# Softmax attention on one Trainium2 core: a bound check in place of the row-maximum pass, with scores in four row strips and weighted sums in four column strips

## The chip, the cores and the metric

The kernel runs on one core of one Trainium2 chip. The metric is the device time of one execution in microseconds (us). On one core there is no second die to compare with, so a run is called fast when it lies within 1.5% of the fastest run of the same kernel; a kernel that was run only once has the state "unknown". All matrices are fp32. The profile also gives the clock that the throttle granted to TensorE, as a share of full speed. Its lines name the engines: PE is a matmul on TensorE and PEld a weight load, DVE is VectorE, ACT is ScalarE, POOL is GpSimd, SP is SyncE. A row strip is a quarter of TensorE's array, 32 of its 128 rows; a column strip is 32 of its 128 columns. In a line, `32*128` is the rows and columns of the array that a matmul uses.

## The reference, cut to what matters

The network takes x of (2, 128, 64, 64) through four residual layers. Layers 1 and 2 (convolutions, and a quaternion product in the Fourier domain) are the same before and after the change. Layers 0 and 3 contain softmax attention over all S = 64 x 64 = 4096 tokens:

```python
# layer 0: 4 heads of 32 channels, q and k of length 1
q1, q2, k1, k2 = map(l2norm_tokens, (q1, q2, k1, k2))
attn1 = jax.nn.softmax(jnp.einsum('bhnc,bhmc->bhnm', q1, k1) * temperature, axis=-1)
out1 = jnp.einsum('bhnm,bhmc->bhnc', attn1, v)
# ... a second attention over channels, output convolutions

# layer 3: 8 heads of 16 channels
a = jnp.einsum('bhcq,bhck->bhqk', q, k) / jnp.sqrt(jnp.float32(C))
a = jax.nn.softmax(a, axis=-1)
o = jnp.einsum('bhqk,bhck->bhcq', a, v)
```

A softmax usually subtracts each row's greatest score, so that the exponentials can't overflow. Its result is the same without the subtraction, as long as no exponential and no sum of them overflows or vanishes.

`l2norm_tokens` divides by `sqrt(sum(t*t, axis=2))`, where axis 2 is that of the tokens: each channel, not each token, has length 1 over the 4096 tokens. For one channel no product of a q and a k exceeds 1, so a score of layer 0 is at most 32 times the temperature, which is 1 here.

## The kernel before

Keys are taken in 32 tiles of 128, queries in 8 blocks of CH = 512 columns (one PSUM bank in fp32). For each head a score matmul puts 128 keys x 512 queries into PSUM, ScalarE takes the exponential into SBUF, and a sum matmul multiplies it with the values, and with ones for the softmax's denominator.

A head needs only 16 or 32 rows of contraction, but every score matmul contracts all 128 rows: q stands in a block that is zero in the rows of the other heads. A first pass over all scores finds the row maxima, which then enter the scores as one more row of the contraction.

```python
def _max_pass(nc, pool, ps_pool, ident, blocks, q, k, hs, d, nh):
    # ... for each query tile qt, key chunk kc and pair of heads p:
                ps = ps_pool.tile([128, 2, CH], F32, tag="sp", name="ps_max")
                for jj in range(2):
                    nc.tensor.matmul(ps[:, jj, :], qm[:, p + jj, :],
                                     k[:, kc * CH : (kc + 1) * CH], start=True, stop=True)
                nc.vector.tensor_reduce(pm[:, p : p + 2, qt, kc], ps, AX.X, ALU.max)
    # ... the maxima are turned and written into a row of q

def _attn_pass(nc, p_pool, ps_pool, acc_pool, blocks, q, k, values, hs, d, nh, done):
    # ... multiply(qb, kt, p, w): two sum matmuls, in different column strips of one accumulator
    for qb in range(NCH):
        # ... qm: q of this block, zero in the rows of the other heads
        for kt in range(NQT):
            for p in range(0, nh, 2):
                ps = ps_pool.tile([128, 2, CH], F32, tag="sp", name="ps_s")
                for jj in range(2):
                    nc.tensor.matmul(ps[:, jj, :], k[:, kt * 128 : (kt + 1) * 128],
                                     qm[:, p + jj, :], start=True, stop=True)
                w = p_pool.tile([128, 2, CH], F32, tag="weights", name="weights")
                nc.scalar.activation(w, ps, AF.Exp)
                waiting.append((qb, kt, p, w))
                if len(waiting) > 1:
                    multiply(*waiting.pop(0))
```

The generators are woven: in layer 0 the maxima pass of the first half with the convolutions for the values, and later maxima passes with the attention pass before them. PSUM, into which the matmuls write, is used as eight banks: three score buffers of two banks each, and two accumulators.

## Time and profile before

| | before |
|---|---|
| median time, us (3 runs) | 16939.77 (16937.05 to 16952.22) |
| TensorE busy | 97% |
| ScalarE busy | 21% |
| VectorE busy | 29% |
| layer 0 / layers 1 and 2 / layer 3, us of the profiled run | 5860 / 1426 / 9684 |

TensorE is the bound. The lines of the profile, and what they say, stand in the prediction below.

### The profile page before, as it was taken

To read this page: it belongs to the slowest core of one execution; us is meant where nothing else is said; L and a number is where in the kernel's file an instruction comes from. 1 tells how busy PE (TensorE), PEld (TensorE's weight loads), DVE (VectorE), ACT (ScalarE), POOL (GpSimd) and SP (SyncE) were. 2 spreads that over 40 slices of the span, in tenths; PEclk is the share of its full clock that TensorE was granted. 3 is DMA by queue.
4 is the path that set the end of the run, shared out by engine and by line. 5 is a ranking of instruction groups with operands and counts; after the bars stand their busy time and mean duration, and the time that the engine had idled before them with its cause. 6 is when DMAs were issued, how large, how long until landed. Compare 5 with 4: busy or idle time off the path is not lost.

```text
span 16969.8 us, 116126 instructions
## 1 busy us (share of the span) xinstructions
PE 16401.0 (97%) x50778; PEld 6151.0 (36%) x50778; DVE 4966.5 (29%) x4328; ACT 3536.5 (21%) x3820; POOL 468.1 (3%) x1029
## 2 busy tenths in 40 slices
PE   8999998999999788899999999999999999999999
PEld 3433322443332246644333333333333333333222
DVE  4432201352320352267422222322223222221000
ACT  1022232102223201100122222222222222222333
POOL 0000000000000100000000000000000000000000
PEclk9999998999999887889999999999999999999999
DMA  0000000000000015400000000000000000000000
GB/s 19 0 0 0 0 0 0 0 0 0 0 1 0 2 17 83 68 2 0 1 1 1 1 1 1 1 1 1 1 1 1 1 1 1 1 1 1 1 1 1
DMA packets 142859, 90.89 MB, mean 5 GB/s; under 512 B 4752, under 2 KB 137616, under 8 KB 142352
## 3 DMA queue, kind: packets, MB, share of 16 engines
q1 hardware_dynamic: 141056, 80.52, 2.9%
q8 instruction: 399, 6.54, 0.2%
q10 hardware_dynamic: 1296, 2.95, 0.1%
q14 instruction: 108, 0.88, 0.0%
HBM read 78.87 MB, written 4.19 MB: 5 GB/s over the span
## 4 chain that ended last, share of the span: by engine, by line
PE 63%; ACT 1%; issue 1%; DVE 0%; POOL 0%; ACTq 0%; DMA 0%; DVEq 0%; POOLq 0%; SPq 0%
PE ps_max L175 22%; PE ps_s L224 21%; PE ps_acc L207 12%; PE ps_freq L735 2%; PE ps_bank L718 1%; PE ps_bank L707 1%; PE ps_bank L614 1%; PE ps_t L585 1%; ACT yt L715 0%; PE ps_bank L622 0%; PE ps_bank L795 0%; PE ps_bank L764 0%; PE ps_bank L572 0%; PE ps_bank L668 0%; PE ps_sp L887 0%
## 5 line engine op out<-in xcount | busy, mean ns | idle before, releaser
L182 DVE TENSOR_REDUCE max_part<-ps_max 128x2 f32<-128x1024 f32 x3072 | 3765.1, 1226 | 7590.7 <-PE ps_max L175 7589.5
L224 PE MATMUL ps_s<-q_block,k 128*128 128x512 f32 x12288 | 5888.7, 602 | 18.6 <-POOL q_block L163 18.6
L175 PE MATMUL ps_max<-k,max_block 128*128 128x512 f32 x12288 | 5842.6, 610 | 11.2 <-ACT weights L232 5.9
L232 ACT ACTIVATE weights<-ps_s 128x1024 f32<-128x1024 f32 x3072 | 3144.9, 1024 | 10551.5 <-PE ps_s L224 10551.4
L175 PEld LDWEIGHTS ps_max<-k,max_block 128*128 128x128 f32 x12288 | 2164.5, 189 | 3662.1 <-issue 2459.3
L224 PEld LDWEIGHTS ps_s<-q_block,k 128*128 128x128 f32 x12288 | 2253.2, 190 | 3313.2 <-issue 2870.5
L207 PE MATMUL ps_acc<-weights,vt 128*32 128x512 f32 (+1 forms) x12288 | 3258.9, 609 | 1.7 <-ACT weights L232 1.7
L207 PEld LDWEIGHTS ps_acc<-weights,vt 128*32 128x32 f32 (+1 forms) x12288 | 497.5, 116 | 2331.9 <-issue 2310.4
L311 PE MATMUL ps_acc<-xn,wc 128*128 128x512 f32 x1440 | 631.3, 594 | 0.0
L470 DVE RECIPROCAL rec<-rec 64x512 f32<-64x512 f32 x32 | 107.0, 3345 | 1468.2 <-ACT rec L469 1468.2
L163 POOL COPY max_block<-q 16x128 f32<-16x128 f32 (+1 forms) x768 | 233.4, 304 | 9288.2 <-PE ps_max L175 8846.6
L885 DVE COPY u<-ps_acc 128x512 f32<-128x512 f32 x32 | 22.1, 690 | 1482.8 <-PE ps_acc L207 1482.8
L311 PEld LDWEIGHTS ps_acc<-xn,wc 128*128 128x128 f32 x1440 | 272.4, 190 | 342.1 <-issue 342.1
L718 PE MATMUL ps_bank<-consts,yt 128*128 128x99 f32 x1024 | 185.5, 338 | 86.2 <-ACT yt L715 86.2
L735 PEld LDWEIGHTS ps_freq<-e,w_r 128*32 128x32 f32 x4224 | 255.8, 153 | 19.0 <-issue 12.7
L735 PE MATMUL ps_freq<-e,w_r 128*32 128x16 f32 x4224 | 259.9, 212 | 2.2 <-DVE e L725 2.2
L735 PE MATMUL ps_freq<-e,w_i 128*32 128x16 f32 x4224 | 255.4, 212 | 0.0
L735 PEld LDWEIGHTS ps_freq<-e,w_i 128*32 128x32 f32 x4224 | 253.0, 157 | 2.8 <-issue 1.4
L163 POOL COPY q_block<-q 17x512 f32<-17x512 f32 (+1 forms) x192 | 115.8, 609 | 4833.5 <-PE ps_s L224 3802.4
L718 PEld LDWEIGHTS ps_bank<-consts,yt 128*128 128x128 f32 x1024 | 160.6, 239 | 219.1 <-ACT yt L715 218.9
L607 DVE SCALAR_TENSOR_TENSOR X<-g,w,X 128x4096 f32<-128x4096 f32 x50 | 234.7, 4693 | 1.8
L725 DVE COPY e<-ps_bank 128x396 f32<-128x396 f32 x128 | 143.4, 1120 | 307.6 <-PE ps_bank L718 307.6
(176 smaller groups left out, 3012.2 us busy)
## 6 DMA issues: line engine op xcount, KB each, us to landing
w_r<-in_L_conv_kr_w SPq DMA_DIRECT2D x16, 528.0 KB, 12.3
w_r<-in_L_conv_kr_x SPq DMA_DIRECT2D x16, 528.0 KB, 11.8
w_r<-in_L_conv_kr_y SPq DMA_DIRECT2D x16, 528.0 KB, 11.9
w_r<-in_L_conv_kr_z SPq DMA_DIRECT2D x16, 528.0 KB, 11.9
w_i<-in_L_conv_ki_w SPq DMA_DIRECT2D x16, 528.0 KB, 5.4
w_i<-in_L_conv_ki_x SPq DMA_DIRECT2D x16, 528.0 KB, 7.7
w_i<-in_L_conv_ki_y SPq DMA_DIRECT2D x16, 528.0 KB, 10.0
w_i<-in_L_conv_ki_z SPq DMA_DIRECT2D x16, 528.0 KB, 11.9
```

The lines of the kernel that those rows point to most:

```text
L163: nc.gpsimd.tensor_copy(block[hs * j : hs * j + rows, j, :], q[hs * j : hs * j + rows, cols])
L175: nc.tensor.matmul(ps[:, jj, :], qm[:, p + jj, :], k[:, kc * CH : (kc + 1) * CH], start=True, stop=True,)
L182: nc.vector.tensor_reduce(pm[:, p : p + 2, qt, kc], ps, AX.X, ALU.max)
L207: nc.tensor.matmul(acc[0][r : r + hs, :], values(kt, p + jj), w[:, jj, :], start=(kt == 0), stop=(kt == NQT - 1),)
L224: nc.tensor.matmul(ps[:, jj, :], k[:, kt * 128 : (kt + 1) * 128], qm[:, p + jj, :], start=True, stop=True,)
L232: nc.scalar.activation(w, ps, AF.Exp)
L311: nc.tensor.matmul(out, wc[:, t, grp * C : (grp + 1) * C], xn[:, c * ROWS + t // 3 : (c + 1) * ROWS + t // 3, t % 3 : t % 3 + W], start=(t ...
L585: nc.tensor.matmul(t3[:, lo // 4, : (hi - lo) * C], xt[:, 3 + u, :], xt[:, u + lo : u + hi, :].rearrange("p k c -> p (k c)"), start=(u == ...
L607: nc.vector.scalar_tensor_tensor(xi, g[:, i : i + H, j : j + W], w8[:, s : s + 1], xi, ALU.mult, ALU.add)
L614: nc.tensor.matmul(pv, t9[:, k, :], t2[:, c * ROWS + k : (c + 1) * ROWS + k, 2 : W + 2], start=(k == 0), stop=False,)
L718: nc.tensor.matmul(pe[:, r * 3 * FW : (r + 1) * 3 * FW], yt[:, r * 128 : (r + 1) * 128], k["fwd_w" if fh == m else "fwd_w_mirror"], start= ...
L735: nc.tensor.matmul(out.rearrange("p (x c) -> p x c", c=2), ws[n][:, :, gq * FW + fw], ef[:, :, 1 - n : 3 - n], start=(n == 0), stop=(n == 1),)
```

## The change

The intent is to spend less TensorE time per head. First, the maxima pass goes. An upper bound of the scores is computed on the device instead (32 x |temperature| in layer 0; in layer 3 the largest |q| times the largest |k| of each channel, summed over a head). If it is over 60, a branch at the end runs the old kernel as the general path and overwrites the output. On the given inputs the bound is 32 in layer 0 and at most 21.6 in layer 3, so the branch isn't taken.

Second, no zero-padded q: four heads lie 32 rows apart, and each score matmul contracts only its own 32 rows. The four matmuls of a turn use four row strips of the array and write to four PSUM banks. Third, the sums use four column strips of 32, four heads at once. The core of the diff, with cuts marked:

```diff
+LIMIT = 60.0
+def _attn_four(nc, p_pool, ps_pool, q, k, multiply):
+    waiting = []
+    for qb in range(NCH):
+        for kt in range(NQT):
+            ps = [ps_pool.tile([128, 2, CH], F32, tag="sp", name="ps_s") for _ in range(2)]
+            for j in range(4):
+                rows = slice(32 * j, 32 * j + 32)
+                nc.tensor.matmul(
+                    ps[j // 2][:, j % 2, :],
+                    k[rows, kt * 128 : (kt + 1) * 128],
+                    q[rows, qb * CH : (qb + 1) * CH],
+                    start=True, stop=True,
+                )
+            w = []
+            for p in range(2):
+                w.append(p_pool.tile([128, 2, CH], F32, tag="weights", name="weights"))
+                nc.scalar.activation(w[p], ps[p], AF.Exp)
+            waiting.append((qb, kt, w))
+            if len(waiting) > 1:
+                multiply(*waiting.pop(0))
...  layer 0: values and ones in two accumulators
+            for n in range(2):
+                for j in range(4):
+                    rows = slice(32 * j, 32 * j + 32)
+                    nc.tensor.matmul(
+                        accs[n][rows, :],
+                        ones if n else vt[:, kt, rows],
+                        w[j // 2][:, j % 2, :],
+                        start=(kt == 0), stop=(kt == NQT - 1),
+                    )
...  layer 3: values and ones of a head share one strip of 32 columns
+            for j in range(4):
+                i = j % 2
+                nc.tensor.matmul(
+                    acc[0][32 * j : 32 * j + 32, :],
+                    vt[:, kt, 2 * t + j // 2, i : i + 2, :].rearrange("p a d -> p (a d)"),
+                    w[j // 2][:, i, :],
+                    start=(kt == 0), stop=(kt == NQT - 1),
+                )
...  layer 3: the bound, once for each sample and half of the heads
+        nc.vector.tensor_reduce(mq, q, AX.X, ALU.max, apply_absolute_value=True)
+        nc.vector.tensor_reduce(mk, k, AX.X, ALU.max, apply_absolute_value=True)
+        nc.vector.tensor_mul(mq, mq, mk)
+        ps = sp()
+        nc.tensor.matmul(ps[:, 0, 0:1], head_sum, mq, start=True, stop=True)
...  the end of the kernel
+            nc.vector.tensor_scalar(within, top, LIMIT, None, ALU.is_le)
+    ok = nc.values_load(within[0:1, 0:1])
+    with tc.If(ok == 0):
+        _general(tc, a, out)
```

A "turn" below is one key tile with four heads in the changed kernel: four score matmuls, two exponentials of 128x1024, and the sums of the turn before (four matmuls in layer 3, eight in layer 0).

## The prediction

> **What bounds the kernel now.** I read the busy shares first, then the chain that ended last, then the costliest groups, then a table of the span by stage, and last the order of time inside one attention loop. The page:
>
> ```profile
> PE 16401.0 (97%) x50778; PEld 6151.0 (36%) x50778; DVE 4966.5 (29%) x4328; ACT 3536.5 (21%) x3820; POOL 468.1 (3%) x1029
> ...
> PE 63%; ACT 1%; issue 1%; DVE 0%; POOL 0%; ACTq 0%; DMA 0%; DVEq 0%; POOLq 0%; SPq 0%
> ...
> L182 DVE TENSOR_REDUCE max_part<-ps_max 128x2 f32<-128x1024 f32 x3072 | 3765.1, 1226 | 7590.7 <-PE ps_max L175 7589.5
> L224 PE MATMUL ps_s<-q_block,k 128*128 128x512 f32 x12288 | 5888.7, 602 | 18.6 <-POOL q_block L163 18.6
> L175 PE MATMUL ps_max<-k,max_block 128*128 128x512 f32 x12288 | 5842.6, 610 | 11.2 <-ACT weights L232 5.9
> L232 ACT ACTIVATE weights<-ps_s 128x1024 f32<-128x1024 f32 x3072 | 3144.9, 1024 | 10551.5 <-PE ps_s L224 10551.4
> L207 PE MATMUL ps_acc<-weights,vt 128*32 128x512 f32 (+1 forms) x12288 | 3258.9, 609 | 1.7 <-ACT weights L232 1.7
> ```
>
> TensorE is busy 97% and hardly waits; VectorE and ScalarE wait for it. Three groups hold 15.0 of 17.0 ms: the scores for the row maxima (L175), the scores again for the softmax (L224), the weighted sums (L207). The program has 24 head-samples (4 heads x 2 in layer 0, 8 x 2 in layer 3), each 8 query blocks x 32 key tiles = 256 score matmuls, 6144 in all; the trace has 12288, so one fp32 matmul is two passes. The stages (start:end, length, then each engine's busy us; PEclk and DMA last):
>
> ```profile
> 0.00:229.00 229.00, 164.66 (x338) 66.51 (x338) 81.50 (x100) 41.69 (x84) 27.05 (x21) 1.00 0.10 35
> 229.00:880.00 651.00, 646.10 (x1622) 294.00 (x1622) 323.33 (x280) 42.41 (x93) 26.43 (x74) 1.00 0.00 0
> 5860.00:6272.00 412.00, 331.36 (x809) 153.60 (x808) 270.14 (x129) 19.33 (x34) 84.92 (x36) 0.87 0.01 2
> 6272.00:7286.00 1014.00, 840.30 (x10696) 643.61 (x10696) 255.44 (x396) 131.41 (x242) 0.97 (x3) 0.74 0.45 70
> 7311.00:8189.00 878.00, 878.00 (x2047) 388.74 (x2046) 628.47 (x516) 0.00 (x0) 33.47 (x116) 1.00 0.00 0
> 15450.00:16960.00 1510.00, 1499.72 (x4127) 424.58 (x4128) 41.38 (x37) 524.08 (x512) 19.28 (x32) 1.00 0.01 1
> ```
>
> Layer 0 ends near 5860, layers 1 and 2 take 412 + 1014 = 1426 us, layer 3 is 7286 to the end, 9684 us. The row 7311:8189 is a pure maxima pass: 878 us / 2048 = 0.429 us a pass, so a full fp32 score matmul costs 0.858 us. The last row is a pure attention pass; inside it:
>
> ```profile
> 16899.68 1.98 PE L224 MATMUL ps_s<-q_block,k 128*128 128x512 f32 x4
> 16900.22 0.19 PEld L224 LDWEIGHTS ps_s<-q_block,k 128*128 128x128 f32 x1 [0.24 <-issue]
> 16901.59 0.14 PEld L207 LDWEIGHTS ps_acc<-weights,vt 128*32 128x32 f32 x4 [0.76 <-issue]
> 16901.60 1.05 PE L207 MATMUL ps_acc<-weights,vt 128*32 128x512 f32 x4
> 16901.76 1.02 ACT L232 ACTIVATE weights<-ps_s 128x1024 f32<-128x1024 f32 x1 [1.87 <-PE ps_s L224]
> 16902.58 0.30 PEld L224 LDWEIGHTS ps_s<-q_block,k 128*128 128x128 f32 x2 [0.84 <-PE ps_s L224]
> ```
>
> One turn (two heads of a key tile) runs 16899.68 to 16902.58, 2.90 us. Two score matmuls are 4 passes x 0.43 = 1.72. The two sums, in different 32-column strips, have 4 passes in 1.05 us including about 0.16 of pipeline tail: two strips run at once, 0.86 for both. The remaining 2.90 - 1.72 - 0.86 = 0.32 is two changes of array shape, drain and first weight load included. ScalarE works 1.02 and waits 1.87.
>
> **What the Trainium skill says.** "TensorEngine Tiling (Array Packing)", Key Properties: tiles load weights and multiply independently, but changing the tiling mode drains the engine. The trace agrees: the strips above overlap, and 0.32 us goes at the two changes. "TensorE: Matmul & The Clock Gate", Part 3: four row tiles of K=32, N=512 measured 3.07 times faster, three column tiles 2.38; a K=32 matmul alone costs what a K=128 one does. No run here shows row tiles yet, nor four strips at once, nor fp32 in them. "PSUM — Partial Sum Buffer", bank collisions: different row tiles must not write one bank at a time; the changed code gives each of the four strips its own bank, and then has room for only one and a half turns (six score banks). "ScalarE: Activation LUTs", What ACT_TABLE_LOAD costs: 186 ns + 0.833 ns an element is 1.04 us for 1024, less some 93 ns when back to back; the trace has 1.024, and where a 0.60 us ACTIVATE has a follower at once, that one starts 0.49 to 0.50 us later. So an exponential stream can run at 0.93 to 1.02 us apiece.
>
> **The change, part by part.** I evaluated the bound on the given inputs: 32 in layer 0 and at most 21.6 in layer 3, under the limit of 60. The branch is not taken, so the general path costs only a flag test, some 10 us.
>
> 1. *Maxima pass removed.* 6144 x 0.858 = 5272 us of TensorE, all on its path; VectorE's 3765 us of reductions and the zero-padded blocks go too, worth nothing by themselves. Layer 0's convolutions for the second attention and the values were woven into the first maxima pass (229:880): 651 - 512 x 0.858 = 212 us of them stays and stands alone now, with some waits: 240 a sample.
>
> 2. *Scores from four row strips.* A turn is now four heads of a key tile. If the strips overlap, four score matmuls cost 0.86 us, not 3.43. An unknown is the weight load: 128 columns take 0.11 us from one start to the next (two loads within 0.30 us, one is 0.19). Four strips loading in parallel add nothing; eight loads strictly one after another would make 0.75 + 0.86 = 1.6. I take 1.0, near parallel.
>
> 3. *Sums from four column strips.* Layer 3: four at once 0.86. Layer 0: values and ones apart, eight matmuls, two rounds, 1.72.
>
> 4. *Turns.* Layer 0: 1.0 + 1.72 + 0.32 = 3.04, TensorE bound; with small waits 3.1; 2 x 256 turns = 1587. Layer 3: TensorE 1.0 + 0.86 + 0.32 = 2.18; ScalarE two exponentials, 1.86 to 2.05; and a loop through both: end of an exponential, sums 0.92, shape change 0.2, scores 1.0 and 0.26 latency, two exponentials, together 4.24 to 4.43 over two turns, 2.1 to 2.2 each. All three nearly agree; I take 2.25; 4 x 256 turns = 2304.
>
> 5. *Edges of layer 3.* Each of 32 query blocks ends with a copy, two selecting matmuls and a reciprocal of 3.36 us that holds one of three score buffers, so about two turns run short. Before it cost 1510/8 - 64 x 2.90 = 3 us a block; now I estimate 5: 160. Each of four half-layers needs its projections unhidden (16 us, as at 7295 to 7311 before) and a new abs-max of q and k, which the built order puts before the first score: 29 each, 116. Statistics, normalizing and values per sample 28: 56. Sum 332; layer 3 is 2304 + 332 = 2636.
>
> 6. *Rest of layer 0.* First prologue 229; woven work now alone 2 x 240; output projections 2 x 118 (2827 to 2945 before); second sample's normalizing and convolutions 67 + 124; block edges 16. Sum 1152; layer 0 is 1587 + 1152 = 2739, against 5860.
>
> Total 2739 + 1426 + 2636 + 10 = 6811 of span; the timed runs are about 30 us below the profiled one, so about 6790, rounded to 6800. TensorE drops from 16.4 ms to perhaps 6; ScalarE stays at 3.4 and becomes a second bound in layer 3.
>
> **Rivals.**
> - *Strips overlap fully and exponentials run back to back.* Turns 2.05 and 2.9: 1024 x 0.2 + 512 x 0.2 = 307 less, about 6500. For it: strips in pairs begin within 0.01 us above. Against: in-order TensorE and only three score buffers of two banks.
> - *Weight loads serialize.* Scores 1.6 a turn: 1536 x 0.6 = 920 more at worst, part hidden in layer 3 by ScalarE: 7400 to 7700. For it: the 0.11 us spacing, which is for one row group; against: the skill's 3.07 times.
> - *Strips run only in pairs.* The profile shows two strips, never four. Sums then cost 1.72 in layer 3 and 3.44 in layer 0: 1024 x 0.86 + 512 x 1.72 = 1760 more, 8500. If the scores paired too, another 1300.
> - *ScalarE becomes the bound and the weaving is missed.* The unwoven parts together cost about what rows 1, 5 and 6 say; if waits doubled them, 300 to 400 more.
>
> **Range and chances.** The maxima alone are 31% of the time, and even the pairs-only case is far below 16940. Main doubt is how well four fp32 strips overlap. 6800 with 6350 to 7700 for 8 in 10: the low end is the first rival with smaller edges, the high end the second. Faster by 2% 0.98, within 0.01, slower 0.01 (the branch taken or a failure).
>
> **What would show it.** In the changed profile: no maxima group and no large reduction; score matmuls of form 32*128, still 12288, four starting nearly together; 16384 sums of form 128*32. A turn in layer 3 near 2.2 us with exponentials 1.0 us apart, one in layer 0 near 3.0 with ScalarE waiting about a third. Layers 1 and 2 at 1426. ScalarE busy near 3.5 ms, over half of the span. Wrong if the four strips' starts are 0.1 us or more apart (weight loads), if third and fourth sums start 0.43 us after the first (pairs), if the granted clock falls below 1.0 in the attention stages, or if a turn in layer 3 has TensorE and ScalarE both idle.

## The result, and the profile after

The changed kernel is correct and takes **6548.69 us** (median of 4 runs, 6520.2 to 6567.97), against 16944.6 for the kernel before in the same rounds. The ratio is 0.3864, with a 95% interval of 0.3854 to 0.3873. Here and below a ratio is the mean time of one kernel's fast runs over that of the other's fast runs of the same rounds, so it isn't quite the ratio of the quoted medians. The prediction of 6800 was 4% too high, and the result lies inside its range.

From the page of the changed kernel: each engine's busy time and share, then the costliest attention groups (count, then busy us and mean ns of one, then the idle time before them):

```profile
PE 5979.5 (91%) x42571; PEld 2201.9 (34%) x42571; DVE 1148.3 (18%) x1183; ACT 3273.5 (50%) x3628; POOL 87.6 (1%) x56
...
L945 ACT ACTIVATE weights<-ps_s 128x1024 f32<-128x1024 f32 x3072 | 2979.5, 1021 | 1009.9 <-PE ps_s L935 950.5
L935 PE MATMUL ps_s<-q,k 32*128 32x512 f32 x12288 | 1918.1, 644 | 28.8 <-DVE o L1300 22.5
L1280 PE MATMUL ps_acc<-weights,vt 128*32 128x512 f32 x8192 | 1131.0, 609 | 0.7 <-ACT weights L945 0.7
...
L1159 PE MATMUL ps_acc<-weights,vt 128*32 128x512 f32 x4096 | 546.3, 605 | 0.0
L1159 PE MATMUL ps_acc<-weights,ones 128*32 128x512 f32 x4096 | 534.0, 592 | 0.0
```

The maxima group and its reductions are gone. The score group still has 12288 records (one for each pass) of about 0.64 us, but it keeps TensorE busy for 1918 us, where it took 5889 before: records of one mean length add up to a third of the time only if they lie on top of one another. That is why the busy column, and not count times mean, has to be read for strips. ScalarE has as many exponentials as before, and its share rises from 21% to 50%.

The table by stage of the changed kernel (start:end, length, then busy us of PE, PEld, DVE, ACT and POOL; the granted clock, DMA share and GB/s last). The stages are the attention of layer 0's first sample, its output projections, layer 1, layer 2, and the attention of layer 3:

```profile
439.00:1189.00 750.00, 749.74 (x6148) 187.50 (x6145) 43.70 (x37) 496.91 (x513) 0.21 (x1) 1.00 0.00 1
1189.00:1297.00 108.00, 57.40 (x70) 16.17 (x65) 43.92 (x28) 16.25 (x25) 0.00 (x0) 0.61 0.00 0
...
2572.00:2980.00 408.00, 329.36 (x808) 153.01 (x808) 268.06 (x129) 19.33 (x34) 85.30 (x36) 0.88 0.01 2
2980.00:3972.00 992.00, 820.14 (x10676) 630.84 (x10676) 259.18 (x402) 130.69 (x241) 0.00 (x0) 0.75 0.46 72
...
4020.00:6534.00 2514.00, 2441.23 (x16684) 658.53 (x16684) 243.30 (x232) 1989.72 (x2051) 0.00 (x0) 0.98 0.01 3
```

Layer 0 ends at 2572 (5860 before), layers 1 and 2 take 408 + 992 = 1400 (1426 before), layer 3 takes 6546 - 3972 = 2574 with the flag at the end (9684 before). So layer 0 gave 3288 us and layer 3 gave 7110 us of the 10423 by which the profiled span fell.

One turn of layer 0's attention and the start of the next, in order of time (start, length, engine, line, operation, count of records; in brackets the idle time before and what ended it):

```profile
801.27 0.31 PEld L935 LDWEIGHTS ps_s<-q,k 32*128 32x128 f32 x8 [0.84 <-issue]
801.27 1.14 PE L935 MATMUL ps_s<-q,k 32*128 32x512 f32 x8
...
802.34 1.07 PE L1159 MATMUL ps_acc<-weights,vt 128*32 128x512 f32 x8
802.51 1.94 ACT L945 ACTIVATE weights<-ps_s 128x1024 f32<-128x1024 f32 x2 [0.99 <-PE ps_s L935]
...
803.23 1.04 PE L1159 MATMUL ps_acc<-weights,ones 128*32 128x512 f32 x8
...
804.20 1.14 PE L935 MATMUL ps_s<-q,k 32*128 32x512 f32 x8
```

Eight weight loads fit in 0.31 us: the four row strips load in parallel. The eight score passes are done in 1.14 us, of which the next matmul waits for only 1.07. Four column strips take 0.89 from the values' start to that of the ones, with no change of shape between. One turn is 804.20 - 801.27 = 2.93 us (2.925 over a whole block: blocks lie 93.6 us apart, which is 32 turns). TensorE never stops, and ScalarE waits 0.99 of it.

In layer 3 the sums are half as many, and the turn has another form:

```profile
5501.93 1.14 PE L935 MATMUL ps_s<-q,k 32*128 32x512 f32 x8
...
5503.00 1.07 PE L1280 MATMUL ps_acc<-weights,vt 128*32 128x512 f32 x8
5503.16 4.01 ACT L945 ACTIVATE weights<-ps_s 128x1024 f32<-128x1024 f32 x4 [0.59 <-PE ps_s L935]
5503.99 0.54 PEld L935 LDWEIGHTS ps_s<-q,k 32*128 32x128 f32 x8 [0.84 <-PE ps_s L935]
5503.99 1.37 PE L935 MATMUL ps_s<-q,k 32*128 32x512 f32 x8
...
5505.30 1.07 PE L1280 MATMUL ps_acc<-weights,vt 128*32 128x512 f32 x8
...
5506.29 1.14 PE L935 MATMUL ps_s<-q,k 32*128 32x512 f32 x8
```

Turns of 2.07 us (5501.93 to 5503.99, rounded) and of 2.30 us (to 5506.29) alternate. In every second turn the scores take 1.37 us and not 1.14, and their weight loads 0.54 and not 0.31: one half of the strips starts about 0.23 us after the other. What holds them is the question of experiments 4, 6, 7 and 9.

### The profile page after: what moved, and what is told of

It is laid out like the page before. It is cut to its first block, busy times and chain, and to the rows that moved or that the text cites. A ratio compares the mean times of both kernels' runs of the same rounds, so it can differ in the third digit from the quotient of the medians.

```text
span 6546.6 us, 94115 instructions
## 1 busy us (share of the span) xinstructions
PE 5979.5 (91%) x42571; PEld 2201.9 (34%) x42571; DVE 1148.3 (18%) x1183; ACT 3273.5 (50%) x3628; POOL 87.6 (1%) x56
## 4 chain that ended last, share of the span: by engine, by line
PE 53%; DVE 3%; ACT 2%; issue 1%; POOL 0%; ACTq 0%; DMA 0%; SPq 0%; DVEq 0%; POOLq 0%
PE ps_s L935 18%; PE ps_acc L1280 16%; PE ps_freq L735 4%; PE ps_bank L718 3%; PE ps_bank L707 2%; DVE rec L1298 2%; PE ps_bank L614 1%; PE ps_t L585 1%; ACT yt L715 1%; PE ps_bank L622 1%; PE ps_bank L795 1%; PE ps_bank L764 1%; PE ps_bank L572 1%; PE ps_bank L668 1%; PE ps_sp L1295 0%
## 5 line engine op out<-in xcount | busy, mean ns | idle before, releaser
L945 ACT ACTIVATE weights<-ps_s 128x1024 f32<-128x1024 f32 x3072 | 2979.5, 1021 | 1009.9 <-PE ps_s L935 950.5
L935 PE MATMUL ps_s<-q,k 32*128 32x512 f32 x12288 | 1918.1, 644 | 28.8 <-DVE o L1300 22.5
L1280 PE MATMUL ps_acc<-weights,vt 128*32 128x512 f32 x8192 | 1131.0, 609 | 0.7 <-ACT weights L945 0.7
L935 PEld LDWEIGHTS ps_s<-q,k 32*128 32x128 f32 x12288 | 605.4, 184 | 1354.1 <-issue 854.7
L1159 PE MATMUL ps_acc<-weights,vt 128*32 128x512 f32 x4096 | 546.3, 605 | 0.0
L1159 PE MATMUL ps_acc<-weights,ones 128*32 128x512 f32 x4096 | 534.0, 592 | 0.0
L1280 PEld LDWEIGHTS ps_acc<-weights,vt 128*32 128x32 f32 x8192 | 166.1, 108 | 813.0 <-issue 781.7
L715 ACT COPY yt<-ps_bank 128x512 f32<-128x512 f32 x128 | 75.0, 586 | 376.9 <-PE ps_bank L707 376.9
L1159 PEld LDWEIGHTS ps_acc<-weights,ones 128*32 128x32 f32 x4096 | 133.3, 110 | 306.4 <-issue 306.4
L1159 PEld LDWEIGHTS ps_acc<-weights,vt 128*32 128x32 f32 x4096 | 81.0, 108 | 388.6 <-issue 376.8
```

The source lines that it names most:

```text
L715: nc.scalar.copy(yt, pt)
L935: nc.tensor.matmul(ps[j // 2][:, j % 2, :], k[rows, kt * 128 : (kt + 1) * 128], q[rows, qb * CH : (qb + 1) * CH], start=True, stop=True,)
L945: nc.scalar.activation(w[p], ps[p], AF.Exp)
L1159: nc.tensor.matmul(accs[n][rows, :], ones if n else vt[:, kt, rows], w[j // 2][:, j % 2, :], start=(kt == 0), stop=(kt == NQT - 1),)
L1280: nc.tensor.matmul(acc[0][32 * j : 32 * j + 32, :], vt[:, kt, 2 * t + j // 2, i : i + 2, :].rearrange("p a d -> p (a d)"), w[j // 2][:, i, :],
```

## The experiments

Experiments 1 to 4 are on one chip, where the kernel before took 16921.74. Numbers 5 to 8, 9 and 10, and 11 are calls on one chip each, timed in 3, 3 and 5 rounds against the kernel before (medians 16945.24, 16930.89 and 16943.28). Differences under 30 us between calls aren't read: the changed kernel itself was 6548.69 in one call and 6523.84 in another.

### 1. Only the maxima pass removed

The kernel before, without its maxima passes and without the maximum's row in q:

```diff
-        _own_rows(nc, qm, q, slice(qb * CH, (qb + 1) * CH), hs, d + 1, nh)
+        _own_rows(nc, qm, q, slice(qb * CH, (qb + 1) * CH), hs, d, nh)
-            _weave(top(0), channels_and_values(), 4)
+            for _ in channels_and_values():
+                pass
-        _weave(attend(b, 0, *qk[-2], vt), top(*qk[-1]), 1)
+        for _ in attend(b, 0, *qk[-2], vt):
+            pass
```

> The kernel before without its passes for row maxima (no shift in the exponent), everything else of it kept: zero-padded full-height scores, sums in pairs of strips. Results stay right, the bound being met. Theory (TensorE time simply adds up): 6144 score matmuls of 0.858 us go, 5272 us, and nothing else moves, as the woven work keeps its own time: 16945 - 5272 = 11670, say 11600 to 11850, still TensorE above 95%. Rival (part of the maxima passes lay beside work that now stands exposed): above 12200.

Measured: 11616.39 us, correct. That is 16921.74 - 11616.39 = 5305 us less; the prediction's term for this part was 6144 x 0.858 = 5272. TensorE's time alone explains the fall to within 33 us, so VectorE's 3765 us of reductions, which went with it, were worth little or nothing by themselves.

### 2. Row strips undone

The changed kernel, with the scores contracting all 128 rows of zero-padded q again:

```diff
+        qm = blocks[qb % len(blocks)]
+        _own_rows(nc, qm, q, slice(qb * CH, (qb + 1) * CH), 32, 32, 4)
-                    k[rows, kt * 128 : (kt + 1) * 128],
-                    q[rows, qb * CH : (qb + 1) * CH],
+                    k[:, kt * 128 : (kt + 1) * 128],
+                    qm[:, j, :],
```

> The changed kernel with the scores back on the full array (q zero-padded to 128 rows by GpSimd, one head at a time), sums still in four column strips. Theory (four row strips run at once, their weight loads too): scores of a turn cost 4 x 0.858 = 3.43 us in place of about 0.95, so a turn costs 2.4 to 2.5 us more: 6549 + 1536 x 2.45 = 10300, between 10100 and 10500. Rival (row strips overlap only in part, weight loads or exponentials already set the turn): 9000 or less.

Measured: 10270.65 us, correct: 3722 more than the changed kernel. Per turn that is 3722 / 1536 = 2.42 us. That is a mean over two stages. In layer 0 blocks lie 175.52 us apart where the changed kernel has 93.6: 2.56 a turn. In layer 3 a turn is 4.63 us and was 2.1825: 2.44. Four full score matmuls are 4 x 0.858 = 3.43 us, so in layer 0 four strips cost 3.43 - 2.56 = 0.87, hardly more than one matmul. The turn of layer 3 in the changed kernel also holds 0.11 of a wait that experiments 7 and 9 find, which a longer turn hides.

### 3. Column strips undone

Sums with all 128 columns, four heads one after another into the same accumulator. The result is wrong on purpose: the heads are mixed.

```diff
-    ones = one.tile([128, 32], F32, name="ones")
+    ones = one.tile([128, 128], F32, name="ones")
-                        accs[n][rows, :],
-                        ones if n else vt[:, kt, rows],
+                        accs[n],
+                        ones if n else vt[:, kt, :],
-                    acc[0][32 * j : 32 * j + 32, :],
-                    vt[:, kt, 2 * t + j // 2, i : i + 2, :].rearrange("p a d -> p (a d)"),
+                    acc[0],
+                    vt[:, kt].rearrange("p g a d -> p (g a d)")[:, 0:128],
```

> The changed kernel with every sum on the full array of 128 columns, all heads into one accumulator (wrong results on purpose), scores still in four row strips. Theory (four column strips run at once): layer 3 pays 4 x 0.858 = 3.43 us a turn in place of 0.86, layer 0 6.86 in place of 1.72: 6549 + 1024 x 2.57 + 512 x 5.15 = 11800, between 11500 and 12000. Rival (column strips overlap only two at a time): half as much more, about 10000 for layer 3 alone at pairs: below 10300.

Measured: 11717.33 us, 5169 more. By passes the estimate is (3.43 - 0.86) x 1024 = 2632 in layer 3 and twice that for half as many turns in layer 0, again 2632, less about 118 for the alternation of layer 3, which a longer turn would hide: 5146. So four column strips run as four at once, not in pairs. Experiments 2 and 3 together are more than the 5068 between experiment 1 and the changed kernel (11616 - 6549), because the kernel before already ran its sums in pairs of column strips.

### 4. Two score buffers in place of three

```diff
-    spp = ctx.enter_context(tc.tile_pool(name="f3_sp", bufs=3, space=PSUM))
+    spp = ctx.enter_context(tc.tile_pool(name="f3_sp", bufs=2, space=PSUM))
```

The same edit was made in layer 0.

> The changed kernel with two score buffers in place of three, in both attention layers. Theory (a turn of layer 3 is set by the loop through score buffers: two row strips have to wait until an exponential frees theirs): with one buffer less the scores split into two halves that no longer overlap, 0.86 us more of TensorE a turn: layer 3 near 2.9 us a turn, layer 0 near 3.7: about 7700, between 7300 and 8000. Rival (TensorE alone, or ScalarE alone, sets the turn and buffers have slack): below 6750.

Measured: 7068.22 us, correct. The direction is the theory's, the size is between both: about 520 to 545 more than the changed kernel. I had taken scores and exponentials of a turn to run one after the other. In the trace the turns of layer 3 alternate, for example between 2.42 and 2.86 us, and the eight score passes last 1.50 and 1.93:

```profile
5499.73 1.50 PE L935 MATMUL ps_s<-q,k 32*128 32x512 f32 x8
...
5502.15 1.93 PE L935 MATMUL ps_s<-q,k 32*128 32x512 f32 x8
...
5505.01 1.50 PE L935 MATMUL ps_s<-q,k 32*128 32x512 f32 x8
```

The first two strips start as soon as *their* buffer is free and the other two follow later. The strips wait separately, so a buffer too few costs only the lag of a half. Buffers matter here; whether three are too few as well was still open.

### 5. The changed kernel again

A control with no edit.

> The changed kernel again, unaltered, as the measure for the three others of this call. All theories: 6520 to 6570 as before, a turn of layer 3 at 2.18 us and one of layer 0 at 2.925.

Measured: 6523.84 us (6517.83 to 6540.91), ratio 0.3852, interval 0.3842 to 0.3861.

### 6. Sums two turns behind the scores

The prediction named a loop through both engines: end of an exponential, sums, change of shape, scores, two exponentials. If the sums' wait for the exponentials closes that loop, one more turn of distance opens it. If the wait is for score buffers, nothing changes.

```diff
-            if len(waiting) > 1:
+            if len(waiting) > 2:
```

> The weighted sums run two turns behind the scores in place of one, so that TensorE does not wait for the newest exponentials before the next scores. Theory (layer 3's 2.18 us is a loop: exponential end, sums, scores, exponentials, over two turns): the loop is cut, the turn falls to what TensorE needs, 2.07: 1024 x 0.11 = 113 us less, about 6440. Rival (ScalarE sets the turn, or the wait is for the score buffers and not for the exponentials' output): no change, 6549. Layer 0 unchanged at 2.925 in both.

Measured: 6541.05 us (6528.33 to 6549.85), ratio 0.3859, correct. That is the control's time within the intervals, and the turns are still 2.07 and 2.30. The loop of the prediction fell.

### 7. One exponential in a turn, the first

ScalarE gets half its work: the second tile's exponential is left out, and its weights are those of the first. Wrong on purpose (relative error 0.029).

```diff
             for p in range(2):
+                if p:
+                    w.append(w[0])
+                    continue
                 w.append(p_pool.tile([128, 2, CH], F32, tag="weights", name="weights"))
                 nc.scalar.activation(w[p], ps[p], AF.Exp)
```

> Only the first exponential of each turn is computed and its result used for all four heads (wrong results on purpose), so that ScalarE has half the work and two of the four scores' banks are never waited for. It measures TensorE's own time of a turn. Theory (TensorE needs 2.07 in layer 3, 2.925 in layer 0): 6549 - 113 - a few for shorter block edges = 6420, between 6380 and 6450; layer 0 unchanged. Rival (ScalarE hides more: TensorE's floor is lower than 2.07): below 6350. Rival (TensorE alone sets 2.18): 6549.

Measured: 6482.26 us (6459.1 to 6491.1), ratio 0.3819, so only some 40 us less than the control and above what was expected. What fell are the ends of the blocks: blocks lie 72.93 us apart and were 74.60, with the same 32 turns in them. In layer 3 of this run ScalarE waits for half of the time, and the alternation is still there:

```profile
5503.59 1.37 PE L935 MATMUL ps_s<-q,k 32*128 32x512 f32 x8
5504.82 1.02 ACT L948 ACTIVATE weights<-ps_s 128x1024 f32<-128x1024 f32 x1 [1.04 <-PE ps_s L935]
...
5505.88 1.14 PE L935 MATMUL ps_s<-q,k 32*128 32x512 f32 x8
...
5507.12 1.02 ACT L948 ACTIVATE weights<-ps_s 128x1024 f32<-128x1024 f32 x1 [1.27 <-PE ps_s L935]
...
5507.95 1.37 PE L935 MATMUL ps_s<-q,k 32*128 32x512 f32 x8
```

So ScalarE's load isn't what sets the turn, and the theory that it is one of three equal bounds fell too. The lines show another loop. A turn takes two of three buffers: turn n writes buffers X and Y, turn n+1 Z and X, turn n+2 Y and Z. So the last two strips of a turn reuse the buffer that the *first* exponential of the turn before reads. The scores start at 5505.88, that exponential ends at 5507.12 + 1.02 = 5508.14, and the strips which start at 5507.95 need it: two of them are late by about 0.2 us, and the scores stretch to 1.37. One exponential is enough to make this loop, provided it is the first.

### 8. The bound's matmul deferred

In each half-layer the changed kernel computes the bound before the first score. Two reductions and a product on VectorE feed a matmul, and TensorE stands still for them. The scores, which don't need the bound, start only after that matmul (4649.14):

```profile
4639.64 4.41 DVE L1245 TENSOR_REDUCE mq<-q 128x1 f32<-128x4096 f32 x1
4643.97 4.41 DVE L1247 TENSOR_REDUCE mk<-k 128x1 f32<-128x4096 f32 x1
...
4648.62 0.59 PE L1250 MATMUL ps_sp<-mq,head_sum 128*128 128x1 f32 x2 [10.35 <-DVE mq L1248]
...
4654.41 1.94 PE L1280 MATMUL ps_acc<-weights,vt 128*32 128x512 f32 x8
```

The wait is 10.35 us, and the sums after it take 1.94 us where 1.07 is normal. That agrees with the Trainium skill, "TensorE: Matmul & The Clock Gate", Part 1: the clock gate halves the array's clock after an idle window and releases it only after a busy one. In the trace the granted clock is 0.50 for 17.07 us, from 4642.09, within the wait, to 4659.15, 10.5 us after TensorE went on. The edit keeps the products and does all the head sums in one matmul at the end:

```diff
-        nc.vector.tensor_mul(mq, mq, mk)
-        ps = sp()
-        nc.tensor.matmul(ps[:, 0, 0:1], head_sum, mq, start=True, stop=True)
-        n = 1 + 2 * b + t
-        nc.vector.tensor_copy(worst[:, n : n + 1], ps[:, 0, 0:1])
+        n = 2 * b + t
+        nc.vector.tensor_mul(products[:, n : n + 1], mq, mk)
...
+    ps = sp()
+    nc.tensor.matmul(ps[:, 0, 0 : 2 * B], head_sum, products, start=True, stop=True)
+    nc.vector.tensor_copy(worst[:, 1 : 1 + 2 * B], ps[:, 0, 0 : 2 * B])
```

> The bound's products of greatest |q| and |k| are kept and summed over the heads by one matmul after the last attention, in place of a matmul before each half-layer's first scores. Theory (TensorE stood idle 10.3 us before each of four half-layers for VectorE's two reductions, and then ran some microseconds at a lower granted clock): 4 x 10 to 15 us less, 6490 to 6510, and the first sums of a half-layer take 1.07 us at once in place of 1.94. Rival (the idle time moves to another wait at the same place): no change.

Measured: 6471.8 us (6468.36 to 6474.56), ratio 0.3818, correct: 52 us less than the control, 13 for each of four half-layers, as expected; only the expected 6490 to 6510 was counted from 6549 and not from this control. The wait was 10.35 of it. The trace supports the half clock as the rest: between the two halves of the first sample the last block of one and the first of the other lie 104.63 us apart in the control, with 17.07 us at half clock in between, and 89.82 here, with none.

### 9. One exponential in a turn, the second

The counterpart of experiment 7. The one exponential that stays now reads the second tile. The first tile's buffer, which the last two strips of the next turn reuse, is never read.

```diff
             for p in range(2):
-                w.append(p_pool.tile([128, 2, CH], F32, tag="weights", name="weights"))
-                nc.scalar.activation(w[p], ps[p], AF.Exp)
+                if p == 0:
+                    continue
+                one = p_pool.tile([128, 2, CH], F32, tag="weights", name="weights")
+                nc.scalar.activation(one, ps[p], AF.Exp)
+                w = [one, one]
```

> As the run with one exponential a turn (6482 us, layer 3 turns still alternating 2.07 and 2.30), but the one that stays reads the second tile, so that the tile which the first two strips write is never read and its buffer is free at once. Wrong result on purpose. Theory (the loop goes through the score buffers: the third and fourth strip of a turn need the buffer that the first exponential of the turn before reads): the alternation goes, layer 3 turns are a flat 2.0 to 2.1, about 1024 x 0.11 = 113 us less: 6350 to 6390. Rival (something that has nothing to do with which buffer is read, for example how fast TensorE's instructions arrive, sets 4.37 us per two turns): unchanged at 6460 to 6500. If the second exponential then holds a buffer that the first two strips of a turn need, it moves by a different amount, and the gap of the strips in the trace will say so.

Measured: 6409.38 us (6393.3 to 6420.61), ratio 0.3786, interval 0.3777 to 0.3796, against 0.3808 to 0.3831 in experiment 7. In layer 3 the alternation is gone:

```profile
5504.12 1.14 PE L935 MATMUL ps_s<-q,k 32*128 32x512 f32 x8
...
5505.41 1.02 ACT L947 ACTIVATE weights<-ps_s 128x1024 f32<-128x1024 f32 x1 [1.04 <-PE ps_s L935]
...
5506.18 1.14 PE L935 MATMUL ps_s<-q,k 32*128 32x512 f32 x8
```

Each turn is 2.07 us and each group of scores 1.14. The number of exponentials is that of experiment 7; only the buffer they read differs. This settles the mechanism: the alternation comes from the score buffers.

The time, though, fell by 73 us and not by the expected 113, and stayed above the expected 6350 to 6390. From the end of the first block to that of the last, layer 3 got only 49 us shorter. A block is 71.43 us and was 72.93: its 32 turns are 32 x 0.115 = 3.7 us shorter, but what it takes beyond its turns grew from 3.0 to 5.2. The rest of the difference isn't from the edit: the stretch of layers 1 and 2 was some 40 us shorter in this profile, at a granted clock of 0.82 and not 0.79, which is also one more reason not to read small differences.

The trace also shows where the block's end gets its price. Four of the score passes after it start 1.04 us late, released by the product that ends the block's normalizing:

```profile
5491.74 3.35 DVE L1301 RECIPROCAL rec<-ps_sp 64x512 f32<-64x512 f32 x1 [2.42 <-PE ps_sp L1299]
...
5495.86 1.13 PE L935 MATMUL ps_s<-q,k 32*128 32x512 f32 x4 [1.04 <-DVE o L1303]
```

At the end of a block two selecting matmuls put the sums and denominators into a score buffer, and it stays taken until reciprocal (3.35 us) and product are done.

### 10. Layer 0's denominators from pre-added exponentials

A version meant to beat both. Layer 0 is bound by TensorE alone, and nearly a third of its turn are the matmuls with ones. With the bound deferred as in experiment 8, VectorE adds the exponentials of four key tiles, and the ones matmuls run once for the four. The edit also moved the last product and addition of each block of layer 0 from VectorE to GpSimd.

```diff
-            for n in range(2):
-                for j in range(4):
...  values and ones, each turn; below, values alone
+            for j in range(4):
...  count(): four ones matmuls on the finished sum of GROUP = 4 tiles
+            if kt % GROUP == 1 and ready:
+                count()
+            if kt % GROUP == 0:
+                held[0] = w
+            elif kt % GROUP == 1:
...
+                first = held[0]
+                held[1] = [
+                    sump.tile([128, 2, CH], F32, tag="sum", name="wsum") for _ in range(2)
+                ]
+                for p in range(2):
+                    nc.vector.tensor_add(held[1][p], first[p], w[p])
+            else:
+                for p in range(2):
+                    nc.vector.tensor_add(held[1][p], held[1][p], w[p])
```

A build with larger pools didn't fit SBUF; the one that ran has three buffers for the added tiles.

> A version meant to beat both: the deferred bound (6472 us) and, in layer 0, the exponentials of four key tiles added on VectorE, so that the four ones matmuls of a turn run only once in four turns. Theory: layer 0 is bound by TensorE alone (turn 2.925, ScalarE waiting 0.99), so three turns of four fall to the 2.18 of the score-buffer loop and one stays at 2.2 to 2.9: mean about 2.37, 512 x 0.55 = 280 us less: 6150 to 6250. VectorE gets six additions of 128x1024 per four turns; from the 1.23 us of the reduction of that size in the kernel before they would take 7.4 of 9.5 us. Rival (VectorE or the weights' buffers, kept longer by the additions, become the bound): turns stay at 2.6 to 2.9 and the time at 6320 to 6470. Correct result, to the reference's tolerance.

Measured: 6244.94 us (6230.47 to 6252.07), ratio 0.3684, interval 0.3675 to 0.3693, correct. That is 227 us less than experiment 8, where 280 was expected. Four turns take 2.07, 2.24, 2.12 and, with the ones matmuls, 3.10 us: a mean of 2.38 where 2.37 was expected. But a block of layer 0 is 78.1 us and was 93.6, which makes 2.44 a turn with the block's end. An addition takes 1.25 us, six of them 7.5 of 9.8 us. VectorE isn't the bound: TensorE is still busy 624 of 630 us there (420 to 1050).

### 11. The score buffer freed early at a block's end

On top of experiment 10, one copy takes both halves out of the score buffer before the reciprocal.

```diff
+            got = two.tile([128, 2, CH], F32, tag="got", name="got", bufs=1)
+            nc.vector.tensor_copy(got[rows], ps[rows])
-            nc.vector.reciprocal(rec[rows, :], ps[rows, 1, :])
+            nc.vector.reciprocal(rec[rows, :], got[rows, 1, :])
-            nc.vector.tensor_mul(o[rows, :], ps[rows, 0, :], rec[rows, :])
+            nc.vector.tensor_mul(o[rows, :], got[rows, 0, :], rec[rows, :])
```

> The version with pre-added exponentials (6245 us, ratio 0.3684), and at the end of each query block of layer 3 the two selected rows are copied from the score buffer to SBUF before the reciprocal of 3.35 us, so that the buffer is free after one copy (64x1024, an estimate of 1.2 to 1.3 us) and not after reciprocal and product (4.1 us). Theory (at the edges too the score buffers set the pace): the block spacing of 74.6 us falls by 1 to 2.5 us, 32 blocks: 30 to 80 us less, 6165 to 6215, ratio 0.364 to 0.3667. Rival (the edge of 4.8 us is TensorE's own: the selecting matmuls and the changes of shape): unchanged, 6230 to 6255. Correct result.

Measured: **6184.16 us** (6171.35 to 6209.49), ratio 0.365, interval 0.3645 to 0.3655, correct. The end of a block in the trace of this kernel:

```profile
4229.19 1.22 DVE L1334 COPY got<-ps_sp 64x1024 f32<-64x1024 f32 x1 [2.13 <-PE ps_sp L1332]
...
4230.44 3.35 DVE L1336 RECIPROCAL rec<-got 64x512 f32<-64x512 f32 x1
...
4231.15 1.38 PE L935 MATMUL ps_s<-q,k 32*128 32x512 f32 x8
```

The next scores start while the reciprocal runs. Blocks lie 72.68 us apart and were 74.60, so 32 x 1.92 = 61 us, which is the difference of the medians. The clock plays a part too: in the trace of experiment 10 seven spacings within a half-layer hold 3.41 us at a granted clock of 0.50 and are some 1.6 us longer than the rest, here none, so that from first block to last layer 3 is 64 us shorter. VectorE does 1.2 us *more* work for each block, and the kernel is faster: what counted was how long the buffer was held.

## Why the prediction was right or wrong

By its own sum, in us of the profiled span:

| term | predicted | measured | difference |
|---|---|---|---|
| layer 0, 512 turns | 512 x 3.1 = 1587 | 512 x 2.925 = 1498 | -89 |
| layer 0, the rest | 1152 | 2572 - 1498 = 1074 | -78 |
| layers 1 and 2 | 1426 | 1400 | -26 |
| layer 3, 1024 turns | 1024 x 2.25 = 2304 | 1024 x 2.1825 = 2235 | -69 |
| layer 3, the rest, with the flag | 342 | 2574 - 2235 = 339 | -3 |
| sum | 6811 | 6546 | -265 |

The number was in the range, but the first rival, strips that overlap fully and exponentials back to back (about 6500), came nearer than the prediction's 6800. The 26 us of layers 1 and 2 say nothing: the same code differed by some 40 us between the profiles of experiments 7 and 9. Two of the signs of being wrong came up, with small effects. In every second turn of layer 3 two strips start more than 0.1 us after the others, but for want of a buffer and not through the weight loads. And the granted clock of layer 3's stage was 0.98: it was at half speed for 17.07 us around the start of each half-layer (experiment 8).

**Maxima pass removed: right.** 5272 was predicted, experiment 1 gave 5305.

**Row strips: the mechanism was right, the guess a little too large.** The prediction took 1.0 us for four scores if the weight loads run nearly in parallel. They do (eight in 0.31 us), and four scores hold TensorE for 1.07 with a change of shape included. Experiment 2 gives 2.42 us a turn for undoing it, and 3.43 - 1.0 = 2.43 follows from the prediction, but that they agree is luck: layer 0 gives 2.56, which leaves 0.87 for four scores and not 1.0, and only the mean with layer 3's 2.44 meets the guess. The rival of serialized weight loads, 7400 to 7700, is out. (What the prediction says of a single matmul with K=32 stands on the page that it names under "Why this matters for your kernels", not in Part 3; no run here has one.)

**Column strips: right.** Four at once, 0.86 to 0.89 us. The rival of pairs, 8500, is out by experiment 3 and by the group of eight sums in 1.07.

**The turn of layer 0: the mechanism was right, the size too large.** TensorE bounds it, ScalarE waits a third. The term 3.1 had 1.0 + 1.72 + 0.32 = 3.04 and 0.06 for small waits. TensorE doesn't wait, and the scores need 0.88 of the turn if changes and sums are taken as predicted (2.925 - 1.72 - 0.32). That is full overlap, as the first rival had it. This is the largest term of the miss.

**The turn of layer 3: nearly the right number for a wrong reason.** The prediction saw three nearly equal limits, and among them a loop that goes from the exponentials through the sums back to the scores. Experiment 6 takes that loop's distance away and changes nothing. Experiment 7 halves ScalarE's load and the alternation stays. TensorE alone would take 2.07, as experiment 9 shows, so that the 2.18 which the prediction had for TensorE meets the measured mean by luck. The 2.1825 come from the third score buffer being shared between two turns. That loop was in the prediction's view of PSUM ("room for only one and a half turns") but was not made a term of the sum. With the right loop the steady state would have been predicted as 2.07 with some delay in every second turn, and not 2.25.

**The rest of layer 0: too large in small pieces.** The first prologue with the convolutions took 439 (469 predicted), the output projections 108 and 88 (118 each), the block edges nothing at all (16), the second sample's normalizing and convolutions 437 (431). The block edges are free since TensorE is the only bound there, and they take no score buffer.

**The edges of layer 3: right.** 4.76 us a block against 5. Their cause was named in part: the reciprocal that holds a score buffer. Experiment 11 shows that 1.92 of the 4.76 come from this.

**The bound's absolute maxima before the first score: right,** and experiment 8 shows it is worth 52 us to move them. The size is luck in part: of the predicted 29 a half-layer, 16 were the projections and 13 the maxima, while in the trace the wait was 10.35 and the rest fits the half clock behind it, which the prediction didn't have.

**Offset of timed runs:** the prediction took some 20 to 30 us off the span, as the profiled span before was 16969.8 and the timed median 16939.77. Here the median of the timed runs (6549) and the profiled span (6546.6) agree, so nothing had to be taken off.

What stays open: whether the turns of layer 3 can be flat at 2.07 with both exponentials. Experiment 9 did it only by leaving one out, and two exponentials together need 1.94 to 2.05 us of ScalarE, so there would be hardly any slack.

## What to carry to other kernels

When small contractions use a quarter of the array, four row strips and four column strips in fp32 came near to four matmuls for the price of one here, and the weight loads ran beside each other. Here each row strip wrote to a PSUM bank of its own. So count next how many turns the score buffers hold, and follow a buffer from its writer to its last reader and to its next writer, strip by strip: in layer 3 that chain put 0.11 us on top of the 2.07 that TensorE needs for a turn, and 1.92 us on a block's edge. An engine that stands still can cost more than the wait, as its clock came back late (experiment 8). Halving one engine's work in two ways, with different buffers released, told load from buffer; and an additional copy that frees a buffer early can pay for itself.

## What the Trainium skill lacked or had wrong

- "TensorE: Matmul & The Clock Gate", Part 3: its figures are for four row tiles (3.07 times faster) and three column tiles (2.38). The runs here add fp32 and four column strips: undoing the row strips cost 2.56 us a turn in layer 0, so 3.43 us had become 0.87 (3.9 times); four column strips took 0.89 us from start to start where four full matmuls are 3.43 (3.9 times).
- "TensorEngine Tiling (Array Packing)", Key Properties: it says that a change of mode drains the engine, with no figure. In layer 0 a turn has three rounds of 0.858 us and lasts 2.925: 0.35 us in all goes beside streaming, for two changes of shape and the starts of three rounds.
- The same page, Gotcha 1: PSUM Pressure, says that row tiles need different banks. It lacks what follows when a turn takes four of six banks: the strips wait separately for their banks, turns of 2.07 and 2.30 us alternate (experiment 9 made them flat), and with four banks they alternate between 2.42 and 2.86.
